# A selective-scan layer on Trainium2: the next chunk's preparation dealt out anew over sixteen steps

## The chip, the cores and the metric

The kernel runs on one core of one Trainium2 chip. The metric is the device time of one execution in microseconds (us). The core has five engines that matter here, each with a queue of its own that it works off in order: PE (TensorE, matrix products, with PEld for its weight loads), DVE (VectorE), ACT (ScalarE), POOL (GpSimd), and SP (SyncE), which issues the DMA transfers. [...]

## The reference, cut to what matters

A network of four layers works on an image batch of shape (3, 256, 48, 48). The change touches the fourth alone, a selective scan (Mamba) over the 2304 pixels of each image. Of the reference:

```python
xn = (xf - mu) * rsqrt(var + 1e-05) * norm_w + norm_b
x_in, z = split(einsum('blc,dc->bld', xn, in_proj_w))          # 512 channels each
u = silu(depthwise_conv4(x_in) + conv_b)
x_dbl = einsum('bld,ed->ble', u, x_proj_w)                     # dt_raw 16, B 16, C 16
dt = softplus(einsum('blr,dr->bld', dt_raw, dt_proj_w) + dt_proj_b)
A = -exp(A_log)                                                # 512 channels x 16 states
def step(hst, inp):                                            # over the pixels
    hst = hst * exp(dt_t[:, :, None] * A) + dt_t[:, :, None] * B_t[:, None, :] * u_t[:, :, None]
    y_t = einsum('bdn,bn->bd', hst, C_t)
y = (y + u * D_param) * silu(z)
out = einsum('bld,cd->blc', y, out_proj_w)
```

The layer's input, normalised over channel groups, is `x`, and its result is added to the unnormalised input.

## The kernel before

The scan layer starts at line 697. The 2304 pixels of each of three images are cut into six chunks of 384, so there are 18 chunks, worked off one after the other (`todo`, line 744). A chunk has 16 steps: four tiles `m` of 128 inner channels by four groups `g`; the text calls them steps 0 to 15, `j = 4 * m + g`. The program's main loop (line 1024) runs over the 288 steps. One step does this:

- **fill** (line 933) writes dt·u·B of the step after it: DVE makes one half (line 939) from `ps_r`, into which PE has spread the rows (`spread_pe`, line 916, two steps ahead of a new `m`), and POOL the other (line 940) from rows that DMAs have spread (`spread`, line 906, issued in the second step of each `m` for the next one).
- **four scans** on DVE (line 1045), one for each state of the group. Each takes one decay exp(dt·A), which ACT writes to PSUM (line 952). The pool `psd` (line 701) has three buffers, so decays are issued three ahead: behind scan `q` of step `s` the program lists decay `4 * s + q + 3`.
- **the product with C** on POOL (line 1056, tile `hc`, two buffers), and on PE the sum over states of the step before (`add_states`, line 957), which for the first step of an `m` starts with a product with D on the diagonal (line 964).
- in the second step of each `m`, the **gate** on DVE (line 975), which multiplies the finished channel tile before by silu(z) and frees the single PSUM tile `ps_y`.

Beside this the steps carry the preparation of the next chunk. `prepare` (line 762) is a generator; each `yield` ends a portion, and `part` (line 1020) runs one portion. A step has two places for it: one at the head, ahead of `fill` and the scans, one after the product with C. Because of that, ACT work of the first place stands in ACT's queue ahead of the decay of that step's fourth scan. In order, `prepare` does: normalise by group (ACT, line 770); mean over channels (PE, line 778), subtraction (DVE, line 780) and square (ACT); variance (PE, line 787), its root by Ln and Exp (ACT, lines 789 and 790), multiplication (DVE, line 792); `xn` (ACT, line 802); four convolutions of 16 recorded matrix instructions each, one per channel tile (PE, line 823), each followed by an ACT pass with the bias (lines 815 and 829); z in two pairs (PE, line 844) with copies (ACT, line 849); Silu over `u` and `sz` (lines 853 and 854) with a load of the activation table ahead of them and one behind them, back to Exp and Ln (line 748); the product with `x_proj_w` (PE, line 860), its copy and the DMAs that broadcast B and C (lines 865 to 873); and dt in two pairs: product (PE, line 883), Abs, Exp and Ln (ACT), two DVE instructions (lines 894 and 895), a copy (ACT, line 898). At the end two DMAs write `dt` and `dtu` to DRAM (lines 901 and 903), from where `spread` reads them.

In the kernel before, a chunk's preparation starts in step 12 of the chunk two before it and ends in step 11 of the chunk before it. All large products of the preparation, and the output projection (line 988), share one PSUM tile of two banks, `two()` (line 759, pool `psg`, one buffer): each user waits until the one before has been read. The projection of the chunk before is done in steps 2 and 3, and its sum with the residual (`store`, line 996) at the head of step 4.

`keep_order` (line 1081) ties the instructions of PE, DVE, ACT and POOL to the order in which the program lists them. SP isn't tied.

Of the kernel before, what the change touches and what calls it, by code (L numbers as in the profile page):

```python
# [9 lines left out]
F32 = mybir.dt.float32  # L10
I32 = mybir.dt.int32
AF = mybir.ActivationFunctionType
# [65 lines left out]
def net(  # L78
# [31 lines left out]
    def v(name, i=0, n=1):  # L110
        at = VEC_AT[name] + i
        return vec[:, at : at + n]
# [72 lines left out]
    with ExitStack() as l0:  # L185
# [8 lines left out]
        def w(name, at, n):  # L194
            a = W0_AT[name] + at
            return w0sb[:, a : a + n]
# [500 lines left out]
    with ExitStack() as l3:  # L697
# [61 lines left out]
        def two():  # L759
            return psg.tile([P, 2, 512], F32, tag="g", name="ps_g")  # L760

        def prepare(at, before, k):


            b, c = todo[at]
            sc, sh = norm3[b]
            xg = k.xg

            for ct in range(CT):
                nc.scalar.activation(  # L770
                    xg[:, ct, :], xg[:, ct, :], AF.Identity,
                    bias=sh[:, ct : ct + 1], scale=sc[:, ct : ct + 1],
                )
            yield
            p = two()
            pm, pv = p[:, 0, :CH], p[:, 1, :CH]
            for ct in range(CT):
                nc.tensor.matmul(pm, mean2, xg[:, ct, :], start=ct == 0, stop=ct == CT - 1)
            yield
            nc.vector.tensor_tensor(  # L780
                xg, xg, pm.unsqueeze(1).broadcast_to([P, CT, CH]), ALU.subtract
            )
            sq = act.tile([P, CT, CH], F32, name="sq", bufs=1)
            nc.scalar.activation(sq, xg, AF.Square)
            yield
            for ct in range(CT):
                nc.tensor.matmul(pv, mean2, sq[:, ct, :], start=ct == 0, stop=ct == CT - 1)
            yield
            nc.scalar.activation(pv, pv, AF.Ln, bias=epst)
            nc.scalar.activation(pv, pv, AF.Exp, scale=-0.5)  # L790
            yield
            nc.vector.tensor_tensor(
                xg, xg, pv.unsqueeze(1).broadcast_to([P, CT, CH]), ALU.mult
            )
            yield
            xn = k.xn = act.tile([P, CT, CH + DCONV - 1], F32, name="xn")
            if c == 0:
                nc.gpsimd.memset(xn[:, :, : DCONV - 1], 0.0)
            else:
                nc.scalar.copy(xn[:, :, : DCONV - 1], before.xn[:, :, CH:])  # L800
            for ct in range(CT):
                nc.scalar.activation(
                    xn[:, ct, DCONV - 1 :], xg[:, ct, :], AF.Identity,
                    bias=v("norm_b", ct), scale=v("norm_w", ct),
                )
            yield
            yield
            u = k.u = act.tile([P, DI, CH], F32, name="u")
            for m0 in (0, 2):

                p = None
                for j in range(2):
                    m = m0 + j
                    if j:
                        nc.scalar.activation(
                            u[:, m0, :], p[:, 0, :CH], AF.Identity, bias=v("conv_b", m0)
                        )
                    yield
                    if not j:
                        p = two()  # L820
                    for tap in range(DCONV):
                        for ct in range(CT):
                            nc.tensor.matmul(  # L823
                                p[:, j, :CH], wtap[:, tap, ct, m * P : (m + 1) * P],
                                xn[:, ct, tap : tap + CH],
                                start=tap == 0 and ct == 0, stop=tap == DCONV - 1 and ct == CT - 1,
                            )
                    yield
                nc.scalar.activation(
                    u[:, m0 + 1, :], p[:, 1, :CH], AF.Identity, bias=v("conv_b", m0 + 1)  # L830
                )
                if m0 == 0:

                    for _ in range(4):
                        yield

            yield
            sz = k.sz = act.tile([P, DI, CH], F32, name="sz")
            for m0 in (0, 2):
                p = two()  # L840
                for j in range(2):
                    m = m0 + j
                    for ct in range(CT):
                        nc.tensor.matmul(
                            p[:, j, :CH], w("in", ct * 512 + m * P, P), xn[:, ct, DCONV - 1 :],
                            start=ct == 0, stop=ct == CT - 1,
                        )
                yield
                nc.scalar.copy(sz[:, m0 : m0 + 2, :], p[:, :, :CH])
                if m0 == 0:  # L850
                    yield

            nc.scalar.activation(u, u, AF.Silu)
            nc.scalar.activation(sz, sz, AF.Silu)
            exp_ln_tables()
            yield

            p = two()
            for m in range(DI):
                nc.tensor.matmul(  # L860
                    p[:96, 0, :CH], w("x", m * 96, 96), u[:, m, :], start=m == 0, stop=m == DI - 1
                )
            yield
            dbc = act.tile([96, CH], F32, name="dbc")
            nc.scalar.activation(dbc, p[:96, 0, :CH], AF.Identity, bias=ident[:96, DTR : DTR + 1])
            bcd = dram.tile([2, DS, CH], F32, name="bcd")
# [12 lines left out]
            for m0 in (0, 2):  # L879
                p = two()  # L880
                for j in range(2):
                    m = m0 + j
                    nc.tensor.matmul(
                        p[:, j, :CH], dtsb[:, m * P : (m + 1) * P], dbc[: DTR + 1, :],
                        start=True, stop=True,
                    )
                yield
                both = dt[:, m0 : m0 + 2, :]
                nc.scalar.activation(both, p[:, :, :CH], AF.Abs)
                nc.scalar.activation(both, both, AF.Exp, scale=-1.0)  # L890
                nc.scalar.activation(both, both, AF.Ln, bias=1.0)
                yield
                pdt = p[:, :, :CH]
                nc.vector.scalar_tensor_tensor(pdt, pdt, 0.0, both, ALU.max, ALU.add)
                nc.vector.tensor_tensor(
                    dtu[:, m0 : m0 + 2, :], pdt, u[:, m0 : m0 + 2, :], ALU.mult
                )
                nc.scalar.copy(both, pdt)

            k.dtd = dram.tile([P, DI, CH], F32, name="dtd")  # L900
            nc.sync.dma_start(k.dtd, dt)
            k.dtud = dram.tile([P // 2, DI, CH], F32, name="dtud")
            nc.sync.dma_start(k.dtud, dtu[P // 2 :])
            yield

        def spread(k, m):

# [106 lines left out]
        for n in range(3):  # L1014
            decay(n)
        parts = {1: prepare(1, k, chunks[1])}
        for _ in range(8):
            next(parts[1])

        def part(at):  # L1020
            if at in parts:
                next(parts[at], None)

        for s, (at, m, g) in enumerate(steps):
# [3 lines left out]

            if j == 0 and at + 2 <= last:
                fetch(at + 2)  # L1030
            if j == 12 and at + 2 <= last:
                parts[at + 2] = prepare(at + 2, chunks[at + 1], chunks[at + 2])
            mine = at + 2 if j >= 12 else at + 1
            part(mine)
            if at and j == 4:
                store(at - 1, 0)
                store(at - 1, 1)
            if s + 1 < len(steps):
                fill(s + 1)

# [13 lines left out]
            cb = k.bc[1][:, g, :].unsqueeze(1).broadcast_to([P, 4, CH])  # L1054
            hc = tiles[s] = scn.tile([P, 4, CH], F32, name="hc")
            nc.gpsimd.tensor_tensor(hc, hs, cb, ALU.mult)  # L1056
            part(mine)
            if j == 1 and at:
                residual(at - 1)
            if at and j in (2, 3):  # L1060
                project(at - 1, j - 2)
            if g == 1 and s >= 5:
                gate(*steps[s - 5][:2])
            if s:
# [121 lines left out]
```

## Time and profile before

| | |
|---|---|
| median of three runs | 4666.53 us (4665.06 to 4667.51) |
| profiled execution, its own time | 4670.4 us |
| its span, first to last instruction | 4668.6 us |
| first scan of the scan layer | at 3002.6 us |
| one chunk, for example 3467.50 to 3559.59 | 92.09 us |
| the 17 distances from chunk to chunk | 91.3 to 93.2 us |
| distance of two products with C (line 1056), undisturbed | 5.17 us |
| mean of a scan, of a decay | 998 ns, 581 ns |
| mean of POOL's two passes (lines 1056 and 940) | 3442 ns, 1815 ns |
| one activation table load | 1283 ns |

A group's line in the profile gives line, engine, operation and tiles; then the busy time and the mean of one instruction; then how long its engine sat idle just before it, and what ended that. In a timeline, a row starts with the start time and the length of a run of equal instructions; the idle time stands in brackets. Neighbouring instructions of one engine overlap a little at their ends, so that four scans of 998 ns together take 3.73 us.

### The profile page before, as it was taken

To read this page: it belongs to the slowest core of one execution; us is meant where nothing else is said; L and a number is where in the kernel's file an instruction comes from. 1 tells how busy PE (TensorE), PEld (TensorE's weight loads), DVE (VectorE), ACT (ScalarE), POOL (GpSimd) and SP (SyncE) were. 2 spreads that over 40 slices of the span, in tenths; PEclk is the share of its full clock that TensorE was granted. 3 is DMA by queue.
4 is the path that set the end of the run, shared out by engine and by line. 5 is a ranking of instruction groups with operands and counts; after the bars stand their busy time and mean duration, and the time that the engine had idled before them with its cause. 6 is when DMAs were issued, how large, how long until landed. Compare 5 with 4: busy or idle time off the path is not lost. (4 is left out here: it accounts for less than half of the span.)

```text
span 4668.6 us, 47523 instructions
## 1 busy us (share of the span) xinstructions
PE 3832.0 (82%) x18498; PEld 1603.0 (34%) x18498; DVE 2840.0 (61%) x2936; ACT 2205.5 (47%) x3196; POOL 1547.2 (33%) x662
## 2 busy tenths in 40 slices
PE   7999999789999976269999998677787777778774
PEld 4322222332322222135555554332333233223321
DVE  4677767357686732640001111388888888888887
ACT  1577767137776755200000000366656666665663
POOL 0000000000000001000000000288998899899888
PEclk9999999899999976589999998787888788788875
DMA  2000000000000001310000001233334333343332
GB/s 79 3 1 1 1 1 1 0 1 1 1 1 1 1 28 31 124 61 0 0 0 0 21 20 58 62 92 100 87 94 101 96 90 100 89 104 91 88 94 51
DMA packets 122319, 207.65 MB, mean 44 GB/s; under 512 B 20881, under 2 KB 114129, under 8 KB 118370
## 3 DMA queue, kind: packets, MB, share of 16 engines
q1 hardware_dynamic: 122082, 204.50, 16.2%
q8 instruction: 147, 2.41, 0.2%
q14 instruction: 90, 0.74, 0.1%
HBM read 167.94 MB, written 36.27 MB: 44 GB/s over the span
## 5 line engine op out<-in xcount | busy, mean ns | idle before, releaser
L387 ACT ACTIVATE pt<-ps_s 128x1024 f32<-128x1024 f32 (+1 forms) x1080 | 952.4, 937 | 363.7 <-PE ps_s L383 306.9
L1056 POOL TENSOR_TENSOR hc<-hs,bc 128x1536 f32<-128x1536 f32 x288 | 991.3, 3442 | 170.3 <-DVE hs L1045 154.5
L1045 DVE TENSOR_TENSOR_SCAN hs<-ps_da,hst,hs 128x384 f32<-128x384 f32 x960 | 902.6, 998 | 134.1 <-ACT ps_da L952 131.2
L952 ACT ACTIVATE ps_da<-dtr,amat 128x384 f32<-128x384 f32 x1152 | 653.5, 581 | 363.4 <-DVE hs L1045 345.3
L394 DVE TENSOR_TENSOR part<-part,pt 128x2048 f32<-128x2048 f32 (+1 forms) x360 | 747.8, 2077 | 40.7 <-ACT pt L387 9.4
L147 POOL TENSOR_TENSOR rstd<-ve,mhalf 128x2 f32<-128x2 f32 (+1 forms) x26 | 16.1, 623 | 1957.5 <-DVE ve L145 1957.5
L383 PE MATMUL ps_s<-q,kt 32*128 32x512 f32 (+1 forms) x4320 | 645.2, 603 | 13.0 <-ACT pt L387 7.0
L940 POOL TENSOR_TENSOR hs<-dtur,bc 128x768 f32<-128x768 f32 x288 | 522.6, 1815 | 90.8 <-DMA dtr<-dtd 90.8
L362 PE MATMUL acc<-pt,vt 128*32 128x512 f32 (+1 forms) x4320 | 535.5, 565 | 0.0
L637 PE MATMUL ps_c<-xpad,wmix 128*128 128x384 f32 x1296 | 421.0, 487 | 100.4 <-DVE wmix L678 100.4
L637 PE MATMUL ps_c<-xpad,wconv 128*128 128x384 f32 x1296 | 423.9, 490 | 8.9 <-DVE xpad L623 8.9
L823 PE MATMUL ps_g<-xn,wtap 128*128 128x384 f32 x1152 | 416.1, 516 | 15.1 <-DVE ot L996 5.3
L619 ACT ACTIVATE xpad<-x,gsh,gsc 128x2304 f32<-128x2304 f32 x6 | 13.9, 2320 | 820.7 <-DVE gsh L178 578.2
L968 PE MATMUL ps_y<-hc,rep 128*32 128x384 f32 x2304 | 302.6, 611 | 117.1 <-POOL hc L1056 106.6
L383 PEld LDWEIGHTS ps_s<-q,kt 32*128 32x128 f32 x4320 | 216.4, 184 | 449.4 <-issue 256.2
L637 PEld LDWEIGHTS ps_c<-xpad,wmix 128*128 128x128 f32 x1296 | 246.0, 190 | 274.8 <-DVE wmix L678 100.5
L637 PEld LDWEIGHTS ps_c<-xpad,wconv 128*128 128x128 f32 x1296 | 247.2, 191 | 184.0 <-issue 13.7
L823 PEld LDWEIGHTS ps_g<-xn,wtap 128*128 128x128 f32 x1152 | 224.9, 201 | 219.6 <-issue 26.0
L939 DVE TENSOR_TENSOR hs<-ps_r,bc 128x768 f32<-128x768 f32 x288 | 272.0, 944 | 4.6 <-PE ps_r L921 4.6
L647 DVE TENSOR_TENSOR x<-ps_c,x 128x384 f32<-128x384 f32 x36 | 20.1, 558 | 382.5 <-PE ps_c L637 382.5
L649 DVE SCALAR_TENSOR_TENSOR x<-ps_c,vec,x 128x384 f32<-128x384 f32 x36 | 22.2, 618 | 370.5 <-PE ps_c L637 370.5
L613 POOL MEMSET xpad<- 128x100 f32 x12 | 2.6, 216 | 674.7 <-PE ps_c L637 526.8
(180 smaller groups left out, 3543.1 us busy)
## 6 DMA issues: line engine op xcount, KB each, us to landing
dtr<-dtd SPq DMA_DIRECT2D x288, 192.0 KB, 3.8
bc<-bcd SPq DMA_DIRECT2D x144, 192.0 KB, 4.9
dtur<-dtud SPq DMA_DIRECT2D x288, 96.0 KB, 3.0
wconv<-in_we SPq DMA_DIRECT2D x16, 1152.0 KB, 7.4
dtd<-dt SPq DMA_DIRECT2D x18, 768.0 KB, 3.5
xb<-in_x SPq DMA_DIRECT2D x6, 1152.0 KB, 12.0
xc<-in_x SPq DMA_DIRECT2D x18, 384.0 KB, 3.2
xd<-x SPq DMA_DIRECT2D x3, 2304.0 KB, 8.3
```

The costliest lines, as they stand in the source:

```text
L362: nc.tensor.matmul(acc[r, :n], vt[:, mt, g * P + h * HD : g * P + (h + 1) * HD], p[:, h, :n], start=first, stop=last,)
L383: nc.tensor.matmul(s[:, j, :n], kt[r, mt * P : (mt + 1) * P], q[r, :n], start=True, stop=True,)
L387: nc.scalar.activation(p[:, h0 : h0 + 2, :n], s[:, :, :n], AF.Exp)
L394: nc.vector.tensor_tensor(part[:, :, :n], part[:, :, :n], p[:, :, :n], ALU.add)
L637: nc.tensor.matmul(pc[:, :CH].rearrange("p (r c) -> p r c", c=HW), wt[:, ct, tap * 256 + m * P : tap * 256 + (m + 1) * P], xp[:, ct, c * R ...
L823: nc.tensor.matmul(p[:, j, :CH], wtap[:, tap, ct, m * P : (m + 1) * P], xn[:, ct, tap : tap + CH], start=tap == 0 and ct == 0, stop=tap == ...
L939: nc.vector.tensor_tensor(hs[:, 0:2, :], k.ps[:, :, :CH], bb, ALU.mult)
L940: nc.gpsimd.tensor_tensor(hs[:, 2:4, :], k.rows[m][1], bb, ALU.mult)
L952: nc.scalar.activation(da[:, :CH], chunks[at].rows[m][0][:, q, :], AF.Exp, scale=amat[:, col : col + 1])
L968: nc.tensor.matmul(k.y_ps[32 * q : 32 * q + 32, :CH], fold, hc[:, q, :], start=False, stop=g == 3,)
L1045: nc.vector.tensor_tensor_scan(hs[:, q, :], decays[q][:, :CH], hs[:, q, :], 0.0 if todo[at][1] == 0 else state[m, g][:, q : q + 1], ALU.mu ...
L1056: nc.gpsimd.tensor_tensor(hc, hs, cb, ALU.mult)
```

## The change

Four things are changed, all in the scan layer.

1. The portions of `prepare` are dealt out anew. It starts in step 13 instead of 12. Two empty portions follow the first pass, so that the mean, the variance and the square stand in steps 14 and 15, the root and the multiplication in step 0, `xn` and the first convolution in step 1 of the next chunk, the second convolution in step 2, the third and fourth in steps 4 and 5, and their ACT passes in steps 2, 3, 5 and 6.
2. The Silu pass over `u` is alone in step 7. The Silu pass over `sz` is moved out of `prepare` into `gates(k)`, which runs at the head of step 4 of the chunk itself, with a table load before and one after it.
3. The two dt pairs are two steps apart: products in steps 8 and 10, Abs, Exp and Ln in steps 9 and 11. z is projected last, in steps 12 and 13, with copies in steps 13 and 14.
4. Both halves of the output projection are issued in step 3, and the two residual sums (`store`) after step 4's scans instead of ahead of its fill.

Since the preparation of one chunk now ends in step 14 and that of the next begins in step 13, steps 13 to 15 run portions of two generators. For the first chunk, `prepare` runs through ahead of the scans as before, followed by `gates`, and six instead of eight portions of the second chunk's.

```diff
@@ prepare
-            yield
+
+            for _ in range(3):
+                yield
             p = two()
...
@@ prepare, after xn
             yield
-            yield
             u = k.u = act.tile([P, DI, CH], F32, name="u")
-            for m0 in (0, 2):
...
+            for m in range(DI):
+
+                if m % 2 == 0:
+                    p = two()
+                j = m % 2
+                for tap in range(DCONV):
                     for ct in range(CT):
                         nc.tensor.matmul(
+                            p[:, j, :CH], wtap[:, tap, ct, m * P : (m + 1) * P],
+                            xn[:, ct, tap : tap + CH],
...
                 yield
+                nc.scalar.activation(
+                    u[:, m, :], p[:, j, :CH], AF.Identity, bias=v("conv_b", m)
+                )
+                yield
+                if m == 1:
+
                     yield
+                    yield
+
+            yield
             nc.scalar.activation(u, u, AF.Silu)
-            nc.scalar.activation(sz, sz, AF.Silu)
             exp_ln_tables()
             yield
@@ prepare, after a dt pair
                 nc.scalar.copy(both, pdt)
-
+                if m0 == 0:
+                    yield
+                    yield
             k.dtd = dram.tile([P, DI, CH], F32, name="dtd")
...
             yield
+
+            yield
+            sz = k.sz = act.tile([P, DI, CH], F32, name="sz")
+            for m0 in (0, 2):
+                p = two()
...
+                yield
+                nc.scalar.copy(sz[:, m0 : m0 + 2, :], p[:, :, :CH])
+                yield
+
+        def gates(k):
+            nc.scalar.activation(k.sz, k.sz, AF.Silu)
+            exp_ln_tables()
@@ ahead of the loop
         parts = {1: prepare(1, k, chunks[1])}
-        for _ in range(8):
+        gates(k)
+        for _ in range(6):
             next(parts[1])
@@ in the loop, head of a step
-            if j == 12 and at + 2 <= last:
+            if j == 13 and at + 2 <= last:
                 parts[at + 2] = prepare(at + 2, chunks[at + 1], chunks[at + 2])
-            mine = at + 2 if j >= 12 else at + 1
-            part(mine)
+            part(at + 1)
+            if j >= 13:
+                part(at + 2)
             if at and j == 4:
-                store(at - 1, 0)
-                store(at - 1, 1)
+                gates(k)
             if s + 1 < len(steps):
                 fill(s + 1)
@@ in the loop, after the product with C
-            part(mine)
+            if at and j == 4:
+                store(at - 1, 0)
+                store(at - 1, 1)
+            part(at + 1)
+            if j >= 13:
+                part(at + 2)
             if j == 1 and at:
                 residual(at - 1)
-            if at and j in (2, 3):
-                project(at - 1, j - 2)
+            if at and j == 3:
+                project(at - 1, 0)
+                project(at - 1, 1)
```

More of the change, by code (lines that the diff above doesn't have):

```diff
@@ L806, in prepare @@
             yield
-            yield
             u = k.u = act.tile([P, DI, CH], F32, name="u")
-            for m0 in (0, 2):
[L811 to L842, printed above, removed]
+            for m in range(DI):
[3 more added lines that the diff above has]
+                for tap in range(DCONV):
                     for ct in range(CT):
                         nc.tensor.matmul(
-                            p[:, j, :CH], w("in", ct * 512 + m * P, P), xn[:, ct, DCONV - 1 :],
-                            start=ct == 0, stop=ct == CT - 1,
+                            p[:, j, :CH], wtap[:, tap, ct, m * P : (m + 1) * P],
+                            xn[:, ct, tap : tap + CH],
+                            start=tap == 0 and ct == 0, stop=tap == DCONV - 1 and ct == CT - 1,
@@ L847, in prepare @@
                         )
                 yield
-                nc.scalar.copy(sz[:, m0 : m0 + 2, :], p[:, :, :CH])
-                if m0 == 0:
+                nc.scalar.activation(
[3 more added lines that the diff above has]
+                if m == 1:
                     yield
+                    yield
+            yield
             nc.scalar.activation(u, u, AF.Silu)
-            nc.scalar.activation(sz, sz, AF.Silu)
@@ L904, in prepare @@
             yield
+            yield
+            sz = k.sz = act.tile([P, DI, CH], F32, name="sz")
+            for m0 in (0, 2):
+                p = two()
+                for j in range(2):
+                    m = m0 + j
+                    for ct in range(CT):
+                        nc.tensor.matmul(
+                            p[:, j, :CH], w("in", ct * 512 + m * P, P), xn[:, ct, DCONV - 1 :],
+                            start=ct == 0, stop=ct == CT - 1,
+                        )
+                yield
[4 more added lines that the diff above has]
+            exp_ln_tables()
         def spread(k, m):
```

## The prediction

> **What bounds the kernel now.** I read the page first. It gives the last 1,660 us to the scan layer: 288 steps, of which each has four scans on DVE (L1045), four exponentials on ACT (L952, "decays") and two passes on POOL. DVE and POOL are both above eight tenths busy there, so neither row alone says which sets the pace.
>
> ```profile
> L1045 DVE TENSOR_TENSOR_SCAN hs<-ps_da,hst,hs 128x384 f32<-128x384 f32 x960 | 902.6, 998 | 134.1 <-ACT ps_da L952 131.2
> ```
>
> So next I took the busy times of one whole chunk (16 steps; columns: stretch, its length, then PE, PEld, DVE, ACT, POOL), and DVE's waits in it.
>
> ```profile
> 3467.50:3559.59 92.09, 69.86 (x273) 29.29 (x272) 80.93 (x93) 56.59 (x92) 82.90 (x34) 0.83 0.38 95
> ```
>
> ```profile
> DVE hs L1045 <- ACT ps_da L952: 9.2, 4, 4.7
> DVE ot L996 <- PE ps_g L988: 1.7, 1, 1.7
> DVE hs L939 <- PE ps_r L921: 0.2, 1, 0.2
> ```
>
> 80.93 us of work and 11.1 us of waits make the 92.09 us. POOL's 82.90 and its 9.2 us of waits, all for L1045, make the same sum: POOL waits because DVE came late. A chunk therefore lasts as long as DVE's work plus the waits ACT and PE put into it, and not under POOL's 82.9. The reader should see that 9.2 of the 11.1 us are waits for decays.
>
> DVE's order in time shows where they stand (a bracket is idle time before the first instruction of the row).
>
> ```profile
> 3462.04 0.93 DVE L939 TENSOR_TENSOR hs<-ps_r,bc 128x768 f32<-128x768 f32 x1
> 3462.89 3.73 DVE L1045 TENSOR_TENSOR_SCAN hs<-ps_da,hst,hs 128x384 f32<-128x384 f32 x4
> ...
> 3475.90 1.02 DVE L1045 TENSOR_TENSOR_SCAN hs<-ps_da,hst,hs 128x384 f32<-128x384 f32 x1 [0.73 <-ACT ps_da L952]
> ...
> 3483.42 1.02 DVE L996 TENSOR_TENSOR ot<-ps_g,ot 128x384 f32<-128x384 f32 x2 [1.72 <-PE ps_g L988]
> ...
> 3511.80 1.02 DVE L1045 TENSOR_TENSOR_SCAN hs<-ps_da,hst,hs 128x384 f32<-128x384 f32 x1 [4.71 <-ACT ps_da L952]
> ```
>
> An undisturbed step is one fill (L939) and four scans; the next fill starts at 3466.54, so a step costs 4.50. With E for the end of a step's last scan, the next fourth scan could start at E+3.50. The three stops are a convolution's wait in step 2, the output additions that wait for the projection in step 4 (1.72), and the Silu passes in step 8 (4.71). A fourth of 3.37 stands at 3531.09 in step 11, where the second dt product waits on the first; 0.39 falls to a copy of z in step 7 and 0.17 to the spreading product.
>
> ACT explains the mechanism. Its queue is in order, and only three decays fit ahead of the scans; whatever ACT does at the head of a step stands before the decay of that step's fourth scan.
>
> ```profile
> 3474.81 0.58 ACT L829 ACTIVATE u<-ps_g,vec 128x384 f32<-128x384 f32 x1 [3.07 <-PE ps_g L823]
> 3475.29 2.25 ACT L952 ACTIVATE ps_da<-dtr,amat 128x384 f32<-128x384 f32 x4
> ...
> 3505.71 1.28 ACT L853 ACT_TABLE_LOAD   x1
> 3507.01 1.48 ACT L853 ACTIVATE u<-u 128x1536 f32<-128x1536 f32 x1
> 3508.40 1.47 ACT L854 ACTIVATE sz<-sz 128x1536 f32<-128x1536 f32 x1
> 3509.88 1.28 ACT L748 ACT_TABLE_LOAD   x1
> 3511.18 2.25 ACT L952 ACTIVATE ps_da<-dtr,amat 128x384 f32<-128x384 f32 x4
> ```
>
> Line 829 waited 3.07 for a convolution; the decay began 0.48 after it, the scan 0.61 after that (3475.90). So the fourth scan starts 1.12 after the convolution's end (0.03 to start line 829 included). ACT is free at about E+0.70.
>
> ```profile
> 3462.07 6.57 PE L823 MATMUL ps_g<-xn,wtap 128*128 128x384 f32 x16
> 3468.56 0.85 PE L968 MATMUL ps_y<-hc,rep 128*32 128x384 f32 x8
> 3469.35 5.43 PE L823 MATMUL ps_g<-xn,wtap 128*128 128x384 f32 x16
> ```
>
> One channel tile's convolution is 5.43, or 6.57 where it starts at half clock. Between two such groups PE's queue holds the state sums, 0.79 (3468.56 to 3469.35); in the step after a new channel tile begins also the diagonal product, 0.74 (3474.61 to 3475.35), and before the third state step the spreading product, 0.85 (3476.13 to 3476.98).
>
> **The change part by part**, as DVE waits in one chunk. The steps come from counting yields, two calls a step: the preparation now starts in step 13 instead of 12, so its call 9 (xn) is the first of step 1, call 10 (convolution 0) the second, and so on; before, call 7 (xn) was the first of step 15.
>
> Step 2 and 3. Normalisation moves from steps 14 and 15 to steps 0 and 1 of the next chunk. Let step 0 end at 0. L792 goes to 0.86, the two xn passes of line 802 end at 2.25 (2.19 after a scan's end at 3458.95), and convolution 0, formerly started before step 0 ended, starts at 2.3. It comes out of a rest of PE. The rows offer 5.43 (all later ones) and 7.62 (the longest, in chunk 0); I take 7.1, near the 7.12 at 3002.63, which also follows a rest. It ends at 9.4; the fourth scan of step 2 may start at 10.5, while DVE is there at 0.85+4.50+0.44 (gate)+3.50 = 9.3. Wait: 1.2 (0 to 1.75). Then 0.74+0.79+0.85 and 5.43 pass before convolution 1 ends, 7.8 later, so step 3's fourth scan starts 3.3 late against 4.50 a step (2.9 to 3.3).
>
> Step 4. The Silu of sz is now alone: load 1.30, pass 1.48, load 1.30, in starts of rows. The decay starts at E+0.70+4.08, the scan at E+5.40 instead of E+3.50: wait 1.9. The projections now follow each other at the end of step 3; 2 x 2.85 end about 2 us before step 4's last scan, so the additions' wait of 1.72 is gone.
>
> Step 5 and 6. The output additions move behind step 4's scans (0.94 of DVE, the same work). Convolution 2 shares their PSUM tile, and starts at E+1.0 instead of 2.8 after the end of step 3. It ends at E+6.4; the fourth scan of step 5 starts at E+7.55, where DVE is at E+0.94+3.50. Wait: 3.1 (to 4.2 if half clock makes the convolution 6.57). Convolution 3 ends 0.79+5.43 later, DVE comes back after 1.0+0.44+3.50: wait 1.3. Queued behind ACT's stuck u pass are all decays, behind these DVE, behind DVE POOL.
>
> Step 7. Silu of u alone: 1.9 by the same sum, where step 8 lost 4.71 to both passes. z's copies, which cost 0.39, now stand in steps 13 and 14.
>
> [...]
>
> Steps 9 and 11. The first Abs-Exp-Ln (2.45, from 3517.87 to 3520.32) costs 0.1 without a gate's cover. The second dt product has two more calls of room. On PE it stands behind the diagonal product, which waits for the gate of step 9 (E+1.85+0.44, the dt pair on DVE being ahead of it), the sums and the spreading product: 3.64 together in the same place now (3517.81 to 3521.45). At half clock the dt product is 2.92 (3525.06), so it ends at E+8.9; ACT's 2.45 and 0.66 to the scan make E+12.0, where DVE is at E+2.29+4.50+3.50: 1.7. At full clock (2.38 and 1.55) it is ready before ACT asks and 0.1 is lost. PE rests before it, so I take 1.5 (0.1 to 2.4), instead of 3.37.
>
> Steps 13 to 15. z's copies (0.80) and the Identity passes (1.31) stand at one step's head, and the mean product (2.92 at 3535.50, cold) must end before step 15's first DVE instruction. Bounds 0 and 3.5; I take 0.7, nearer the lower end, since the trace loses nothing at its own cold mean product and z's products run just ahead of the new place.
>
> The DMAs move too. Ten issues for bc come a step earlier. The two output stores come 4.6 us later on SP and hold up the rows behind them in that queue; these are needed in step 7, some 8 us after they would land. I cost both at nothing; without that cover up to a few us in step 7.
>
> Sum: 1.2+3.3+1.9+3.1+1.3+1.9+0.1+1.5+0.7 = 15.0 us of waits against 11.16 now: +3.84 a chunk (bounds +0.1 to +9). Seventeen chunks carry a preparation: +65. Before the first step, z's products and copies leave the chain (2947.52 to 2954.99, 7.5), and the Silu of sz, 4.1, stands partly before the first fourth scan: -6. The last chunk prepares nothing; its lone Silu wait falls into DVE's lead of 0.67 a step: 0. The profiled execution lasted 4670.4 (span 4668.6), so 4729; it stands 3.9 above the median 4666.53, which gives **4725.5**.
>
> **Rivals.** A, faster: the u passes do not hold up DVE. Its place is steps 3, 5 and 6, its price their 7.7 us. Before's passes of lines 815 and 829 cost only 0.73 of DVE, and the tile order is the same; against it stands that convolution 2 can't begin before the additions. It decides once 3.9 of the 7.7 are hidden; if all are, -3.9 a chunk: 4725.5-17x7.7 = 4595. POOL's 82.9 allows 4510 at most.
> B, the gains and losses cancel: PE stays at full clock, convolution 0 is 5.43, step 11 and steps 13 to 15 lose 0.1 and 0. Waits 11.3, so 4663. For it: sums and products lie closer together than before. Against: PE came back at half clock from its rests of 3.62 (3525.06) and 4.79 us (3535.50).
> C, the mean product and dt product both come cold: waits near 19.5, 4800. For it, the 2.92 rows; against, z's products run just before the mean product and warm PE.
>
> **How the numbers follow.** Forecast 0.68, A 0.17, B 0.09, C 0.06. The forecast's own range is 4680 to 4785, by the bounds of steps 2, 11 and 13 to 15, which hardly fall all on one side. B and part of A take the low end to 4650: half of A and C stay outside. A measurement tells 0.2% (9 us) from no change: faster 0.17, same 0.09 (B), slower 0.74.
>
> **What would show it.** In the changed profile: chunk length near 95.9; 36 more table loads on ACT; DVE's idle time before scans near 3.1 in step 5 and 1.9 in steps 4 and 7, ended by decays; ACT's wait for convolutions up from 122 us in 3000:4500; step 11 under 3.37; POOL's waits near 13 a chunk. I am wrong if DVE waits under 11 a chunk, if step 5 shows no wait, or if DVE itself waits for the mean product by more than 1 us.

## The result, and the profile after

The changed kernel takes 4712.32 us (median of four runs, 4705.45 to 4716.86) against 4667.02 (four runs, 4665.06 to 4670.41) for the kernel before. The ratio is 1.0095, with a 95% interval of 1.0078 to 1.0113: slower by 45 us, where 4725.5 was forecast and 4650 to 4785 was the range. The profiled execution lasted 4715.86 us (span 4714.1), 45.5 more than the one of before.

The groups of the page come first: the scans, then the convolutions, last the convolutions of the kernel before. The 960 scans work little longer in all, 910.9 against 902.6 us, but DVE's idle time ahead of them rose from 134.1 to 205.1, nearly all of it ended by decays. PE's idle time ahead of the convolutions rose from 15.1 to 70.2, most of it ended by line 996, the output additions.

```profile
L1046 DVE TENSOR_TENSOR_SCAN hs<-ps_da,hst,hs 128x384 f32<-128x384 f32 x960 | 910.9, 1001 | 205.1 <-ACT ps_da L952 199.2
...
L817 PE MATMUL ps_g<-xn,wtap 128*128 128x384 f32 x1152 | 447.4, 547 | 70.2 <-DVE ot L996 42.2
...
L823 PE MATMUL ps_g<-xn,wtap 128*128 128x384 f32 x1152 | 416.1, 516 | 15.1 <-DVE ot L996 5.3
```

An ordinary chunk, in the same columns as before (stretch, length, PE, PEld, DVE, ACT, POOL), then DVE's waits and the longest of POOL's in it:

```profile
3371.10:3466.70 95.60, 70.96 (x272) 30.40 (x272) 81.42 (x93) 60.14 (x108) 83.08 (x34) 0.82 0.38 92
```

```profile
DVE hs L1046 <- ACT ps_da L952: 13.6, 8, 4.5
DVE hs L939 <- PE ps_r L921: 0.4, 2, 0.2
...
POOL hc L1057 <- DVE hs L1046: 11.4, 6, 4.8
```

95.60 us, where 95.9 was forecast and 92.09 stood before. DVE works 81.42 in it (80.93 before) and waits 14.0 (11.1 before); POOL still works 83. So of the 3.5 us by which the chunk grew, some 2.9 are waits of DVE, and 0.5 stand as work: a fourth scan that starts after a wait no longer overlaps the scan before it (2.83 and 1.02 us in the rows, where four scans in a row take 3.73), and there are more such breaks now. The wait for the projection (line 996, 1.7) is gone; the waits for decays are up from 9.2 to 13.6. DVE's order in time shows them by step; only the rows that begin with a wait are shown, and the output additions.

```profile
3380.18 1.02 DVE L1046 TENSOR_TENSOR_SCAN hs<-ps_da,hst,hs 128x384 f32<-128x384 f32 x1 [0.53 <-ACT ps_da L952]
...
3387.81 1.02 DVE L1046 TENSOR_TENSOR_SCAN hs<-ps_da,hst,hs 128x384 f32<-128x384 f32 x1 [2.74 <-ACT ps_da L952]
...
3394.29 1.02 DVE L1046 TENSOR_TENSOR_SCAN hs<-ps_da,hst,hs 128x384 f32<-128x384 f32 x1 [1.87 <-ACT ps_da L952]
3395.22 1.00 DVE L996 TENSOR_TENSOR ot<-ps_g,ot 128x384 f32<-128x384 f32 x2
...
3404.33 1.02 DVE L1046 TENSOR_TENSOR_SCAN hs<-ps_da,hst,hs 128x384 f32<-128x384 f32 x1 [4.50 <-ACT ps_da L952]
...
3410.47 1.02 DVE L1046 TENSOR_TENSOR_SCAN hs<-ps_da,hst,hs 128x384 f32<-128x384 f32 x1 [1.07 <-ACT ps_da L952]
...
3416.95 1.02 DVE L1046 TENSOR_TENSOR_SCAN hs<-ps_da,hst,hs 128x384 f32<-128x384 f32 x1 [1.59 <-ACT ps_da L952]
```

These are steps 2 to 7. Here they stand beside the terms of the prediction (later steps from the same view, further on):

| step | what DVE waits for, through a decay | predicted | measured |
|---|---|---|---|
| 2 | convolution 0 | 1.2 | 0.53 |
| 3 | convolution 1 | 3.3 | 2.74, and 0.18 for the spreading product |
| 4 | Silu of sz with two table loads | 1.9 | 1.87 |
| 5 | convolution 2 | 3.1 (bound 4.2) | 4.50 |
| 6 | convolution 3 | 1.3 | 1.07 |
| 7 | Silu of u with two table loads | 1.9 | 1.59, and 0.18 for the spreading product |
| 9 | first Abs, Exp, Ln | 0.1 | 0.11 |
| 11 | second Abs, Exp, Ln | 1.5 | 0.64 |
| 13 to 15 | copies of z, Identity passes, mean product | 0.7 | 0.70 |
| sum | | 15.0 | 14.1 |

ACT's rows show what stood ahead of the decays:

```profile
3386.72 0.58 ACT L823 ACTIVATE u<-ps_g,vec 128x384 f32<-128x384 f32 x1 [4.79 <-PE ps_g L817]
...
3389.58 1.28 ACT L903 ACT_TABLE_LOAD   x1
3390.87 1.48 ACT L903 ACTIVATE sz<-sz 128x1536 f32<-128x1536 f32 x1
3392.38 1.28 ACT L748 ACT_TABLE_LOAD   x1
3393.67 2.25 ACT L952 ACTIVATE ps_da<-dtr,amat 128x384 f32<-128x384 f32 x4
...
3403.24 0.58 ACT L823 ACTIVATE u<-ps_g,vec 128x384 f32<-128x384 f32 x1 [7.20 <-PE ps_g L817]
```

In steps 3 and 5 ACT stands at the bias pass of line 823 for 4.79 and 7.20 us because the convolution isn't done; all decays are queued behind it. Between 3000 and 4500 us ACT lost 288.1 us in this way, against 122 before. Between steps 3 and 5 stands the Silu of sz: load, pass, load, decay begin 1.29, 1.51 and 1.29 apart. PE's rows show why the third convolution was so late; the last row is the third convolution of the kernel before:

```profile
3387.39 5.43 PE L988 MATMUL ps_g<-sz,w3sb 128*128 128x384 f32 x16
...
3396.27 6.93 PE L817 MATMUL ps_g<-xn,wtap 128*128 128x384 f32 x16 [2.67 <-DVE ot L996]
...
3484.50 5.43 PE L823 MATMUL ps_g<-xn,wtap 128*128 128x384 f32 x16 [0.33 <-DVE ot L996]
```

The projections end at about 3392.8. The third convolution shares their PSUM tile and can't begin until DVE has added both (3395.22 to 3396.22), and these additions stand behind the fourth scan of step 4, which the Silu of sz holds up by 1.87. So PE rests 2.67 us, where it rested 0.33 before, comes back at half clock (the trace grants 0.50 from 3395.92 to 3399.33, then 1.00), and needs 6.93 instead of 5.43.

### The profile page after: what moved, and what is told of

Read it like the earlier page. It is cut to its first block, busy times and chain, and to the rows that moved or that the text cites. A ratio compares the mean times of both kernels' runs of the same rounds, so it can differ in the third digit from the quotient of the medians.

```text
span 4714.1 us, 47569 instructions
## 1 busy us (share of the span) xinstructions
PE 3840.6 (81%) x18498; PEld 1620.0 (34%) x18498; DVE 2846.7 (60%) x2936; ACT 2245.8 (48%) x3232; POOL 1548.8 (33%) x662
## 5 line engine op out<-in xcount | busy, mean ns | idle before, releaser
L1046 DVE TENSOR_TENSOR_SCAN hs<-ps_da,hst,hs 128x384 f32<-128x384 f32 x960 | 910.9, 1001 | 205.1 <-ACT ps_da L952 199.2
L817 PE MATMUL ps_g<-xn,wtap 128*128 128x384 f32 x1152 | 447.4, 547 | 70.2 <-DVE ot L996 42.2
L817 PEld LDWEIGHTS ps_g<-xn,wtap 128*128 128x128 f32 x1152 | 241.1, 215 | 288.5 <-DVE ot L996 53.4
```

Source lines behind the costliest of these rows:

```text
L817: nc.tensor.matmul(p[:, j, :CH], wtap[:, tap, ct, m * P : (m + 1) * P], xn[:, ct, tap : tap + CH], start=tap == 0 and ct == 0, stop=tap == ...
L1046: nc.vector.tensor_tensor_scan(hs[:, q, :], decays[q][:, :CH], hs[:, q, :], 0.0 if todo[at][1] == 0 else state[m, g][:, q : q + 1], ALU.mu ...
```

## The experiments

The theory T on the prediction's grounds: DVE's waits on the in-order queue of ACT make the loss, and the largest part of it comes from the place of the output additions, since the third convolution stands behind them. A rival S says that the 36 more table loads (ACT has 3232 instructions instead of 3196) are what costs. Two smaller questions are what the two chunks of 99.97 us are, and whether it paid to set the dt pairs apart. The expectations name runs by labels of their own: their e4 and e7 are experiments 4 and 7 here, their e8 is experiment 9 and their e9 experiment 10.

**1. The output additions back at the head of step 4.** Nothing else is changed; all loads stay.

```diff
             if at and j == 4:
                 gates(k)
+                store(at - 1, 0)
+                store(at - 1, 1)
...
-            if at and j == 4:
-                store(at - 1, 0)
-                store(at - 1, 1)
```

> The changed kernel with the two residual sums (store) put back ahead of step 4's fill, nothing else. Theory W (the loss comes from ACT's u passes, which wait for convolutions and hold up the decays; the place of the sums makes the third convolution late): DVE waits about 4.1 us for the projections before the sums in step 4, the Silu wait of 1.9 there is hidden behind it, the third convolution starts without a rest of PE and takes 5.43 instead of 6.93, and the waits of 4.5 in step 5 and 1.1 in step 6 fall to nothing. About 3.3 us a chunk, some 4658 us (4650 to 4675). Rival S (the loss is the second Silu pass with its two more table loads, and the sums' place is of no matter): 4712 within 10 us, or more by the 1.7 us a chunk that the sums' wait once cost (4740).

Measured: 4665.88 us (4654.22 to 4668.33), ratio to the kernel before 1.0000 (0.9991 to 1.0010). DVE's waits in a chunk of 92.10 us, then PE's third convolution:

```profile
DVE hs L1048 <- ACT ps_da L952: 6.5, 5, 2.7
DVE ot L996 <- PE ps_g L988: 4.0, 1, 4.0
DVE hs L939 <- PE ps_r L921: 0.2, 1, 0.2
```

```profile
3291.92 5.43 PE L817 MATMUL ps_g<-xn,wtap 128*128 128x384 f32 x16 [0.33 <-DVE ot L996]
```

DVE now waits 4.0 for the projection at the head of step 4, and in exchange the waits of steps 4, 5 and 6 (1.87, 4.50, 1.07) are gone: the Silu of sz runs while DVE waits, PE rests only 0.33 us, the convolution takes 5.43. A wait at the step's head takes the place of three behind it. This one move takes back the whole 45 us, with every load in place: S falls as a cost of the loads wherever they stand, and T holds for the place of the additions. That the time comes out equal to that of the kernel before is partly chance. The start and the first chunk stay short (86.20, 93.24 before); the others lie between 91.1 and 94.4, on the mean 92.7 against 92.1.

**2. The changed kernel without the Silu of sz and its two loads** (the gate then multiplies by z itself).

```diff
         def gates(k):
-            nc.scalar.activation(k.sz, k.sz, AF.Silu)
-            exp_ln_tables()
+            pass
```

> The changed kernel without the Silu pass over sz and its two table loads; the gate multiplies by z instead of silu(z). Theory W: the wait of 1.88 in step 4 goes, and the third convolution may come without a rest of PE (5.43 instead of 6.93), so 1.9 to 3.3 us a chunk, 4655 to 4682 us; the waits of step 3 (2.7), step 5 (3.1 or more) and step 6 (1.1) stay. Rival S: the whole 4.08 us of pass and loads lie on the path in each of 18 chunks, about 4640 us or less.

Measured: 4658.62 us, ratio 0.9984 (0.9974 to 0.9994), chunks of 92.17.

```profile
3288.71 5.43 PE L817 MATMUL ps_g<-xn,wtap 128*128 128x384 f32 x16 [0.68 <-DVE ot L995]
```

Step 4's wait is gone, so the additions come earlier and PE's rest is 0.68 us; the convolution takes 5.43, and step 5 waits 3.0 as the prediction's sum had it. Step 6 keeps its 1.07. So 1.87 of a chunk is the Silu itself with its loads, and 1.5 what it did to PE's clock by way of the additions; both sum to the 3.4 us by which the chunk is shorter. In this order of the program, then, the pass and its loads do cost, and taking them away undoes the loss as well as moving the additions does. Pass and loads were not taken away one without the other.

**3. The memset on DVE.** Chunks 5 and 11, the ones whose successor begins a new image, took 99.97 us instead of 95.6. There the first columns of `xn` are set to zero on POOL (line 800). PE's and then POOL's rows in the changed kernel:

```profile
3470.19 7.51 PE L817 MATMUL ps_g<-xn,wtap 128*128 128x384 f32 x16 [3.71 <-POOL xn L800]
```

```profile
3466.66 3.44 POOL L1057 TENSOR_TENSOR hc<-hs,bc 128x1536 f32<-128x1536 f32 x1
3470.02 0.11 POOL L800 MEMSET xn<- 128x6 f32 x1
```

The memset of 0.11 us stands on POOL behind a product with C, and the convolution waits 3.71 us for it.

```diff
             if c == 0:
-                nc.gpsimd.memset(xn[:, :, : DCONV - 1], 0.0)
+                nc.vector.memset(xn[:, :, : DCONV - 1], 0.0)
```

> The changed kernel with the small memset of xn's first three columns, needed for an image's first chunk, on DVE instead of POOL. Theory W with the POOL queue: the two chunks of 99.97 us, in which the first convolution waited for that memset behind a product with C, become 95.6 us like the others, 8.7 us in all, about 4704; the wait of 3.6 before the fourth scan of step 2 in these chunks falls to 0.5. Rival (these chunks are long for another reason, such as the image's change itself): both stay near 100 us and the time near 4712.

Measured: 4704.31 us, ratio 1.0080 (1.0063 to 1.0096); the two chunks fell from 99.97 to 96.74, step 2's wait in them from 3.6 to 0.53. The cause of the two long chunks is shown: 3.2 us of each, 6.5 together, where the medians differ by 8.0. The 1.1 us that the two keep above 95.6 are not the memset's; step 11 waits 1.91 in them instead of 0.64.

**4. The kernel before, with only the two Silu passes separated:** that of sz goes to the head of step 4, ahead of the additions.

```diff
             nc.scalar.activation(u, u, AF.Silu)
-            nc.scalar.activation(sz, sz, AF.Silu)
             exp_ln_tables()
...
             if at and j == 4:
+                gates(k)
                 store(at - 1, 0)
```

> The kernel before with one part of the change alone: Silu over sz taken out of the preparation and run at the head of step 4 of its own chunk, with its two table loads. Theory W: the wait of 4.71 in step 8 falls by 1.39, the lone pass in step 4 runs beside the sums' wait for the projection and costs nothing; 1.4 us a chunk gained, some 4 us lost ahead of the first step: about 4647 us. Rival S: two more table loads cost 2.6 us a chunk, about 4711 us.

Measured: 4654.00 us, ratio 0.9977 (0.9967 to 0.9986).

```profile
DVE hs L1050 <- ACT ps_da L955: 9.0, 5, 3.4
DVE ot L999 <- PE ps_g L991: 1.7, 1, 1.7
```

Step 8's wait fell from 4.71 to 3.34, and step 4 has the same 1.7 for the projection as before: the Silu of sz is hidden behind it. So the separation by itself is a gain, with 36 loads more, though a small one: 12 us, where 19 were expected. Step 8 gave the 1.4 us a chunk that was expected, but on the mean 0.4 came back as waits for convolutions in steps 1 and 2; the chunk of this view, 92.06 long, is one in which nearly all came back, and on the mean a chunk is 91.2. That the lone pass still costs 3.34 in step 8, and not the 1.9 of the prediction, is in part z's second copy, which stands ahead of the pass in this kernel and which experiment 10 moves.

**5. The dt pairs one step apart again, in the changed kernel.**

```diff
                 nc.scalar.copy(both, pdt)
-                if m0 == 0:
-                    yield
-                    yield
+            yield
+            yield
```

> The changed kernel with the two dt pairs one step apart again (products in steps 8 and 9, two empty portions behind the second pair; z and the dt DMAs stay where the change put them). Theory W: the second product waits for the first pair's copy, so about 3.0 us are waited before step 10's fourth scan and nothing in step 11 (0.64 to 2.1 now): 2 to 2.4 us a chunk, about 4750 us. Rival (the distance is worth nothing because the second product comes at PE's half clock in either place): 4712 within 10 us.

Measured: 4734.02 us, ratio 1.0154 (1.0138 to 1.0171). Step 10 waits 2.90 and step 11 nothing, against nothing and 0.64, so setting the pairs apart takes some 2.2 us of an ordinary chunk out of these two steps; the changed kernel pays 0.70 in step 13, which waits for nothing here. The time rose by only 22 us, where 38 was expected, because of step 13 and since another thing happened to the third convolution:

```profile
3296.72 5.43 PE L817 MATMUL ps_g<-xn,wtap 128*128 128x384 f32 x16 [2.67 <-DVE ot L995]
```

After the same rest of 2.67 us it ran at full clock here, as in 9 of 16 chunks, and step 5 waited 3.01 instead of 4.50; in the other seven it took 6.83 to 8.42. The length of the rest alone does not decide the clock. In the scan layer of the changed kernel's trace the granted clock changes at marks that are 3.413 us, or a multiple of it, apart. Of this rest (3294.05 to 3296.72) 1.82 us lie ahead of the mark at 3295.87; in the changed kernel (3393.60 to 3396.27) 2.32 lie ahead of the mark at 3395.92, from which on half the clock is granted. In all 16 chunks in which the changed kernel's third convolution follows a rest, 2.15 to 2.56 us of it lie between two marks, and the convolution takes 6.91 to 7.12. That the part of a rest between two marks decides the clock is my estimate from these rests; no run shows it.

**6. Convolutions 2 and 3 in steps 3 and 4, the projections in step 6** and their additions ahead of step 7's fourth scan (and the memset on DVE). This tries to take steps 5 and 6 off the path.

```diff
             for q in range(4):
+                if at and j == 7 and q == 3:
+                    store(at - 1, 0)
+                    store(at - 1, 1)
...
-            if at and j == 3:
+            if at and j == 6:
                 project(at - 1, 0)
                 project(at - 1, 1)
```

> The changed kernel with the third convolution in step 3, the fourth in step 4, their u passes in steps 5 and 6 as now, both halves of the output projection in step 6, the residual sums ahead of step 7's fourth scan (where DVE waits for the Silu pass of u anyway), and the memset of xn on DVE. Theory W: no u pass waits in steps 5 and 6 (4.5 and 1.1 us gone), the sums' 0.94 us lie in a wait that is there already, and the waits of step 3 (2.7), step 4 (1.9), step 7 (1.6 less 0.9) stay: some 6.5 us a chunk, 89 us a chunk, about 4600 us (4585 to 4630), faster than both kernels though all 36 added table loads are still there. Rival S (the added Silu pass and loads make the loss): not under the kernel before, 4666.

Measured: 4661.38 us, ratio 0.9989 (0.9980 to 0.9999): a miss by some 60 us. PE's rows, then DVE's:

```profile
3305.30 0.91 PE L973 MATMUL ps_y<-u,diag 128*128 128x384 f32 x2 [1.86 <-DVE sz L984]
3306.14 1.30 PE L977 MATMUL ps_y<-hc,rep 128*32 128x384 f32 x8
3307.38 1.65 PE L930 MATMUL ps_r<-dtu,rep 32*128 32x384 f32 x4
3308.96 7.53 PE L997 MATMUL ps_g<-sz,w3sb 128*128 128x384 f32 x16
```

```profile
3316.53 1.02 DVE L1005 TENSOR_TENSOR ot<-ps_g,ot 128x384 f32<-128x384 f32 x2 [3.18 <-PE ps_g L997]
```

The projections now stood on PE behind the diagonal product, which waits for the gate on DVE (1.86 of rest); the clock was then at half until 3313.24, so the projections took 7.53 instead of 5.43 and DVE waited 3.18 for them. Another 1.20 came in step 5: the bias pass of convolution 2, listed behind convolution 3 here, began only when that one, in the same PSUM tile, was done. Of the 6.5 us a chunk that were to go, 3.4 went; the rest moved.

**7 and 8. Extra DVE work where no wait was expected to take it up.** The thought was: if chunk lengths follow the sum of DVE's work and its waits, added work must show in full; if they are held by something else, it must not. First two products of 384 columns with both inputs in SBUF, in step 8; then one of 768 columns with one input in PSUM.

```diff
+            if j == 8:
+                for i in range(2):
+                    nc.vector.tensor_tensor(
+                        spare[:, i, :], k.u[:, i, :], k.u[:, i + 2, :], ALU.mult
+                    )
```

> The changed kernel with two DVE products of 384 columns into an unused tile in step 8 of every chunk, some 0.9 us of DVE work more. Plain theory (a chunk is DVE's work plus its waits): 0.9 us a chunk more, 96.5 us, 4728 us. Rival (a chunk's length is held to a whole number of the 3.413 us windows in which PE's clock is granted: 95.57 is 28 of them, and the kernel before has 92.1 to 92.2, 27): the chunks stay at 95.57 us, the waits shrink by 0.9, and the time stays at 4712 within 8 us.

Measured: 4821.09 us, ratio 1.0336 (1.0319 to 1.0354): neither. The row of the new tile (count; minimum, median and maximum in ns):

```profile
L1068 DVE TENSOR_TENSOR spare<-u x36: 544/1897/8515, 3038.2 to 4764.0; 128x384 f32<-128x384 f32 x36
```

The products were not 0.54 us each: the median is 1.9 and the longest 8.5, beside POOL's passes. So this run answers another question, and the dose was given again from PSUM:

```diff
+            if j == 8:
+                nc.vector.tensor_tensor(spare, k.ps[:, :, :CH], k.u[:, 0:2, :], ALU.mult)
```

> The changed kernel with one more DVE product of 768 columns in step 8 of every chunk, one input in PSUM like the fill's (so 0.86 us, without the stretching by POOL that two SBUF inputs showed in e7), into an unused tile. Plain theory (a chunk is DVE's work plus its waits): 96.4 us a chunk, about 4727 us. Rival (a chunk's length settles at a whole number of PE's clock windows of 3.413 us): the chunks stay at 95.57 (28 windows, 4712 us within 6) or go to 98.99 (29, about 4767).

Measured: 4718.95 us (4717.94 to 4720.66), ratio 1.0108 (1.0093 to 1.0122), between the two.

```profile
3373.80:3469.40 95.60, 70.32 (x272) 30.15 (x272) 82.12 (x94) 60.22 (x108) 83.00 (x34) 0.82 0.38 92
```

DVE works 82.12 instead of 81.42, the product itself 0.93, and this chunk is 95.60 long again, because its waits came to 13.4 instead of 14.1 (steps 11 and 13 give 0.28 and 0.17 of that, steps 9, 2 and 5 another 0.11, 0.09 and 0.04). In the profiled execution the work did not show; in the medians a part did. So the plan of the experiment was too simple: DVE came later to waits that follow, and these became shorter by as much as its work grew. That needs nothing that holds the chunk's length, but it does not exclude it; the question stays open.

**9 to 11. Further edits on the kernel of experiment 4.** All three put both projections in step 2, and leave the additions at the head of step 4. Experiment 9 also lets the copy of `dt` precede DVE's second dt product; experiment 10 adds that z's second copy stands behind the Silu of u; experiment 11 has that, and the `dt` copy back in its old place.

```diff
@@ all three
-            if at and j in (2, 3):
-                project(at - 1, j - 2)
+            if at and j == 2:
+                project(at - 1, 0)
+                project(at - 1, 1)
@@ the first two
+                nc.scalar.copy(both, pdt)
                 nc.vector.tensor_tensor(
                     dtu[:, m0 : m0 + 2, :], pdt, u[:, m0 : m0 + 2, :], ALU.mult
                 )
-                nc.scalar.copy(both, pdt)
@@ the last two
-                nc.scalar.copy(sz[:, m0 : m0 + 2, :], p[:, :, :CH])
                 if m0 == 0:
+                    nc.scalar.copy(sz[:, m0 : m0 + 2, :], p[:, :, :CH])
                     yield
             nc.scalar.activation(u, u, AF.Silu)
             exp_ln_tables()
+            nc.scalar.copy(sz[:, 2:4, :], p[:, :, :CH])
```

> The split of the Silu passes on the kernel before (e4), with two further edits: the copy of a dt pair is listed ahead of DVE's second product, so that it waits for one DVE instruction instead of two, and both projections stand in step 2. Theory W: the second dt product starts 0.9 us earlier, so step 11's wait falls from 3.37 to about 2.5; the sums' wait in step 4 falls from 1.72 to about 0.9, and the lone Silu pass there stays hidden: 1.7 us a chunk, about 4626 us (4615 to 4640). If the chunk's length is held by PE's clock windows instead, the gain may be anything from 0 to 3.4 us a chunk (4595 to 4654).

> As e8, and z's second copy behind the Silu pass of u and its loads instead of ahead of them. Theory W: the Silu pass no longer waits 0.8 us for z's product, step 8's wait falls from 3.3 to about 2.6, and the x product starts some 2 us later, which costs up to 0.3 in step 9: about 0.5 us a chunk under e8.

> As e9, with the dt pair's copy listed behind DVE's second product again, as in the kernel before. Theory W, corrected by e8 (whichever of the two readers of the dt PSUM tile is listed second waits for the first, so the early copy cost DVE 0.92 twice a chunk and gave 0.83 back in step 11): two waits of 0.92 go, step 11's wait returns from 2.54 to 3.37, about 1.0 us a chunk under e9, some 4626 us (4615 to 4640). Rival (e9's gain came from the early copy): 4654, as e4.

Experiment 9 measured 4657.41 us, ratio 0.9977 (0.9966 to 0.9987), where 4615 to 4640 was expected: no gain on experiment 4. Step 11's wait fell from 3.37 to 2.54 and step 4's from 1.72 to 0.74, but a new wait ate it (DVE's waits, 3000 to 4500 us):

```profile
DVE dtu L895 <- ACT dt L894: 29.4, 32, 0.9
```

The product of line 895 and the copy read the same PSUM tile, and the second in the listed order waits for the first: 0.92 us twice a chunk. Experiment 10: 4643.01 us, ratio 0.9945 (0.9934 to 0.9957); step 8's wait is 2.57 instead of 3.34, and step 9 pays 0.39 on the mean. Experiment 11: 4631.18 us (4626.56 to 4634.23), ratio 0.9920 (0.9907 to 0.9934), the fastest of all and 34 us under the kernel before. A chunk of it, and DVE's waits from 3000 to 4500 us:

```profile
3458.10:3548.40 90.30, 67.91 (x276) 29.29 (x275) 81.17 (x93) 58.89 (x94) 82.94 (x33) 0.87 0.39 97
```

```profile
DVE hs L1051 <- ACT ps_da L956: 139.0, 91, 3.5
DVE ot L1000 <- PE ps_g L992: 12.3, 16, 1.0
```

139.0 us for decays, against 159.3 before and 225.3 in the changed kernel over the same stretch; 12.3 for the projections, against 28.0 before. DVE's work in the chunk is 81.17, against 80.93 before, so the gain lies in the waits.

## Why the prediction was right, and where its terms were off

**The bound** was right: a chunk lasts as long as DVE's work and the waits put into it, 81.4 and 14.0 of 95.60, while POOL's 83 did not set the pace. Work and waits fill the time of any engine; what decides is that no wait of DVE was ended by POOL, while 11.4 us of POOL's waits were ended by scans.

**Step 2** was put too long (1.2, measured 0.53). The convolution starts at 3371.87, 0.6 us earlier than summed, since its first products need only the first of the two `xn` passes (that is how I read the start 0.76 us after the passes begin); its 7.18 after a rest of 0.95 us hit the 7.1 taken.

**Steps 3, 4, 6 and 7** were right to 0.6 us. The lone pass with its loads costs 1.87 and 1.59 where 1.9 was summed.

**Step 5** is the term that was mis-sized: 3.1 taken, 4.50 measured, and even the bound of 4.2 was passed. The order was right (Silu, additions, convolution, decay), but I charged half clock only as a bound, and with 6.57 us, although my own sum gave PE a rest at that place. Experiments 1 and 2 show the price: with rests of 0.33 and 0.68 us the convolution takes 5.43 and not 6.93. Experiment 5 shows that a rest of this length need not bring half clock, so that it did so in every ordinary chunk could not be read from its length.

**Step 11** was too dear (1.5, measured 0.64; 1.9 to 2.1 in chunks 5, 6, 11 and 12). With step 2 it cancels the error of step 5, so the sum of 15.0 against 14.1 is better than its terms, and the 95.9 against 95.60 better still, since DVE's work, which I had left as it was, rose by 0.5. In that the near hit is luck.

**Outside the ordinary chunk** the errors also cancel. The start gave 7.4 back (6 summed). The first chunk I counted like the others, at +3.84, but it has neither additions of an earlier chunk nor a Silu of sz: it fell from 93.24 to 85.64. The two chunks with the memset, at +15.7 together, I had not seen: I followed POOL's big passes, and not the 0.11 us instruction that the moved convolution waits for. Fourteen ordinary chunks at +3.33 make +46.6, the last -1.7; with these the sum is 46.6 + 15.7 - 7.6 - 1.7 - 7.4 = 45.6, against 45.5 between the profiled executions.

**Rival A** (the bias passes do not hold up DVE) fails: steps 3, 5 and 6 cost 8.3 us, not nothing. But experiment 1 shows that most of that, in steps 5 and 6, was a matter of where the additions stand. **Rival B** (gains and losses cancel, with PE at full clock) fails: convolutions 0 and 2 came at 7.18 and 6.93, not at 5.43. Experiment 1 arrives at its number, 4665.88, in another way. **Rival C** fails at step 11, and the mean product held DVE up nowhere: its waits in the chunk are for decays and the spreading product alone. The moved DMAs, which I had put at nothing, ended no wait of DVE or POOL there.

## What to carry to other kernels

On an engine with an in-order queue, a pass that waits for a late product costs what is queued behind it (here ACT's bias pass waited 7.20 us in step 5, and DVE 4.50 behind it); so read for each moved step not only what it takes but what stands behind it, tiny instructions on other engines included (a memset of 0.11 us, and PE's wait of 3.71 for it). When a buffer has one user at a time, try the instruction that frees it ahead of the long work of its engine, even at the price of a wait there: here 4.0 us of wait at the head of step 4 replaced 7.4 behind it. A part of a change that loses as a whole (ratio 1.0095) may still gain: the separated Silu alone gave 0.9977 (0.9967 to 0.9986), and with two edits that the change did not have, both projections in step 2 and z's second copy behind the Silu of u, 0.9920 (0.9907 to 0.9934).

## What the runs showed of the hardware that was not expected

**Chunk lengths in steps.** Many lengths cluster at 92.1 to 92.2 (experiment 2 at 92.17, 6 at 92.15), 95.4 to 95.6 (changed kernel, experiments 3, 5 and 8) and 102.40 (experiment 7); those of the kernel before gather less closely, 91.3 to 92.9 behind the first chunk. In the scan layer of both kernels' traces PE's granted clock changes at distances of whole 3.413 us, and 27, 28 and 30 of these are 92.16, 95.57 and 102.40. In the changed kernel the clock's pattern repeats with the chunk: a half-clock stretch begins at 3300.34 and again at 3395.92, 95.58 later. The same 2.67 us of rest came with 6.93 us in one kernel and with 5.43 in another (experiment 5). That a chunk locks to whole multiples of 3.413 us, because a later start of a convolution meets a different clock, is only argued, and not shown: the lengths of experiments 1, 4 and 9 to 11, the first chunk aside, are spread from 88.9 to 94.4 us without such steps, and what became of the dose of experiment 8 can be told without it.

**A DVE product with two SBUF inputs beside POOL** took 0.54 to 8.5 us (median 1.9), with one input in PSUM and twice the columns it took 0.93. Between experiments 7 and 8, only the form with both inputs in SBUF was stretched. In experiment 7 two of these products took 5.08 us together beside POOL passes of 3.75 and 2.13 us, where the two passes ahead of these took 3.44 and 1.81. The scans, whose decays lie in PSUM, stay near 1 us (1000 ns on the mean) beside POOL's 83 us of work a chunk. What stretches the products was not shown.
